# A four-layer sparse graph network: sums ahead of the tail's steps, reciprocals from PSUM, and the next block's queries at chosen tail steps

## Chip, cores and metric

The kernel runs on one core of one Trainium2 chip. The metric is the device time of one execution in microseconds. Before the change three executions took 2613.1 (median), 2613.42 and 2607.16 us.

## What is computed

Sixteen sequences of 1024 nodes with 128 features pass through four layers, all with one 1024 x 1024 adjacency matrix whose entries are 1 with probability 0.0078 (about 8 neighbours per node). Layers 0, 2 and 3 are masked attention blocks, layer 1 is a graph attention with one score per edge. Biases and norms' gains are inputs.

```python
# attention layer (0, 2, 3); 8 heads of 16
scores = einsum('bnhd,bmhd->bhnm', Q, K) / 4
scores = where(adj == 0, -inf, scores)
out = einsum('bhnm,bmhd->bnhd', softmax(scores), V)
x = layer_norm(h + out @ Wo + bo)
x = layer_norm(x + relu(x @ W1 + b1) @ W2 + b2)

# graph layer (1)
h = x @ W
e = leaky_relu((h @ a_src)[:, :, None] + (h @ a_dst)[:, None, :], 0.2)
y = softmax(where(adj == 0, -inf, e)) @ h + x
x = layer_norm(y)
```

## The kernel before

Nodes are sorted by degree and dealt to 8 row blocks of 128 nodes. The 16 sequences are two groups of 8. A **unit** is one layer, one group and one row block: 4 x 2 x 8 = 64 units, worked through in that order. In this document they are also called blocks. Inside a unit the neighbours of its nodes are taken in **parts**: each part gathers, by indirect DMA on GpSimd (L856), the key and value rows of up to two slots per node. The last part of a unit is a half-filled one, for leftovers ("MIX"). An attention unit has 5 parts, the one of row block 0 has 7.

VectorE does three steps per part: `products` multiplies the gathered keys by the repeated queries (L868, tile pr), `exponentials` reduces over a head (L891), with the exponential on ScalarE (L895), and `weighted` multiplies the gathered values by the exponentials (L919). TensorE sums the weighted rows by node with matmuls against 0/1 matrices `marks`: `summed` (L935, tile acc) for values, two parts at once where they belong to one round. At the end of a unit `divided` sums the exponentials in the same way into a PSUM bank (den), ScalarE copies them (L971, tile both), VectorE takes the reciprocal (L973) and multiplies (L976, tiles o, two halves). GpSimd adds both to `seen`, a check on range.

A unit's **tail** then runs beside the next unit's parts, for both halves h = 0 and 1, the second one step behind. It is a generator of 15 steps in an attention layer:

1. turn o (L596, copy L598) and add the bias to x (L640)
2. output projection into ybanks (L644, L645)
3. squares for the norm's variance, on ScalarE (L580)
4. power -1/2 on GpSimd (L586)
5. scale, ScalarE (L589)
6. turn and evict with gain and shift (L596, L600, tile x)
7. first feed-forward matmuls (L655) and relu (L659)
8. second feed-forward (L664, L668)
9. to 11. squares, power and scale again
12. turn and evict (L600, tile xT)
13. and after: projection to the next layer's keys and values in steps (L538 or L558, copies L542, L559 and their like, then a store). In the last layer there are a second turn (tile outs) and an indirect store by GpSimd (L625) instead.

The steps that hold no matmul are 3 to 5 and 9 to 11.

**Fronts**: `queries(u + 1)` makes the next unit's repeated queries in four steps, for each half a matmul with Wq and its copy (L819, L823), then four matmuls that repeat rows (L828) with four copies (L831, tile qr). **Loads** bring the unit after that, and `slow` is work of layer 0 for the second group.

All of these are written into five in-order instruction queues by one loop over the parts, under a manual schedule: the program's order is the order on each engine. `others()` is called three times per part of an attention layer. Each call adds `pace[1]` to a counter, which advances all tails by a step whenever it reaches 1, and then makes one step of the first of fronts, loads or slow. The pace spreads 15 steps over a unit's calls. In iteration i of the loop, i counts parts; the calls stand as follows before the change: products(i), others, summed(i-2) and perhaps the start of `divided`, exponentials(i), others, weighted(i-1), gathers for part i+3; if a unit is closing, the rest of its tails and the end of `divided`; others.

PSUM has four rotating banks for `bank()`, two ybanks for projections, and one acc. A new bank waits until the readers of the one four allocations earlier are done. A product tile pr has four buffers, so a part's product waits for the sum over the part four earlier.

Lines are those of the kernel before. The change shifts later lines by up to 14.

Of the kernel before, what the change touches and what calls it, by code (L numbers as in the profile page):

```python
# [108 lines left out]
STEPS = 15  # L109
# [13 lines left out]
def sparse_path(ctx: ExitStack, tc: tile.TileContext, a: dict, out: bass.AP, flag):  # L123


    nc = tc.nc
# [71 lines left out]
    val_i, part = some(J, QUADS, dtype=I32), some(J, QUADS, dtype=I32)  # L198
# [559 lines left out]
    units = [(l, g, t) for l in range(len(LAYERS)) for g in range(GR) for t in range(T)]  # L758
    parts = []
# [9 lines left out]
    def is_attention(u):  # L769
        return LAYERS[units[u][0]][1] is ATTN  # L770
# [28 lines left out]
    def queries(u):  # L799

        l, g, t = units[u]
        if not is_attention(u):
            ps = bank([P, J + 1, G])
            for j in range(J):
                nc.tensor.matmul(ps[:, j, :], rep_of(j, True), srcs[g, t], start=True, stop=True)
            for k, j in enumerate(SHARED[t]):
                at = slice(64 * k, 64 * k + 64)
                nc.tensor.matmul(
                    ps[at, MIX, :], rep_of(j, True)[:, at], srcs[g, t], start=True, stop=True
                )  # L810
            ofs[u] = smalls.tile([P, J + 1, G], F32, tag="of", name="of")
            nc.scalar.copy(ofs[u], ps)
            return
        qs[u] = reps.tile([P, J, ROW], F32, tag="qr", name="qr")
        for h in range(HF):
            q = ones_.tile([P, GH * D], F32, tag="q", name="q")
            ps = bank([P, GH, D])
            for i in range(GH):
                nc.tensor.matmul(  # L819
                    ps[:, i, :], xs[l, g, t][:, h, i, :], w[LAYERS[l][0], "Wq"],  # L820
                    start=True, stop=True,
                )
            nc.scalar.copy(q, ps.rearrange("p g d -> p (g d)"))  # L823
            yield
            pss = []
            for j in range(J):
                ps = bank([P, GH * D])
                nc.tensor.matmul(ps, rep_of(j), q[32 * j : 32 * j + 32], start=True, stop=True)  # L828
                pss.append(ps)
            for j in range(J):  # L830
                nc.scalar.copy(qs[u][:, j, h * GH * D : (h + 1) * GH * D], pss[j])  # L831
            yield
# [130 lines left out]
    def divided(u):  # L963

        l, g, t = units[u]
        heads, d = (H, HD) if is_attention(u) else (1, D)
        den = bank([P, G * heads])
        for n, c in enumerate(sum(PIECES[t], [])):
            marked(t, c, den, exs[u][:, n, :])
        both = smalls.tile([P, 2, G * heads], F32, tag="both", name="both")  # L970
        nc.scalar.copy(both[:, 0, :], den)  # L971
        yield
        nc.vector.reciprocal(both[:, 1, :], both[:, 0, :])  # L973
        for h in range(HF):
            o = twos.tile([P, GH, D], F32, tag="o", name="o")
            nc.vector.tensor_tensor(  # L976
                o.rearrange("p g (a d) -> p (g a) d", d=d),
                accums[u][:, h, :].rearrange("p (a d) -> p a d", d=d),
                both[:, 1, h * GH * heads : (h + 1) * GH * heads]
                .rearrange("p (a o) -> p a o", o=1)  # L980
                .to_broadcast([P, GH * heads, d]),
                ALU.mult,
            )
            tails.append((attention_tail if heads > 1 else graph_tail)(l, g, t, h, o))
        n = G * heads
        nc.gpsimd.tensor_tensor(seen[:, :, :n], seen[:, :, :n], both, ALU.add)

    tails = []
    fronts = []
    loads = []  # L990
# [4 lines left out]
            if next(gen, "end") == "end":  # L995
                gens.remove(gen)

    pace = [0.0, 0.0]

    def idle():  # L1000
        return slow if held[0] or not busy[0] else []

    def others():
        pace[0] += pace[1]
        while pace[0] >= 1.0:
            advance(tails)
            pace[0] -= 1.0
        for gens in (fronts or loads or idle(),):
            if not gens:
                continue  # L1010
            got = next(gens[0], "end")
            if got == "end":
                gens.pop(0)
            if got == "idle":
                advance(idle())

    with tc.manual_schedule():
        wide = [gather_buffer() for _ in range(EDGES)]
        setup, entry, weights = graph(wide), at_once(0), load_weights("L0")
        next(setup)  # L1020
        next(weights)
        next(entry)
        more = [weights, load_graph_weights()]
        rest = slots()
        for i, room in enumerate(setup):
            if i == T:
                for gen in more:
                    next(gen)
            if room == "load":
                for _ in loaded(0):  # L1030
                    next(entry, None)
            elif room == "queries":
                for _ in entry:
                    pass
                for _ in queries(0):
                    pass
            elif isinstance(room, str):
                next(rest)
            else:
                for _ in range(room):  # L1040
                    next(entry, None)
        for _ in entry:
            pass
        scratch.close()
        prods = ctx.enter_context(tc.tile_pool(name="prods", bufs=4))
        smalls = ctx.enter_context(tc.tile_pool(name="smalls", bufs=3))
        slow.append(at_leisure(1))
        for i in range(AHEAD - 1):
            gathered(i)
        nc.gpsimd.memset(wide[3], 0.0)  # L1050
        gathered(AHEAD - 1)
        fronts.extend([rest, loaded(1)] + more)
        closing = None
        begun = 0
        for i in range(len(parts) + 2):
            here = i < len(parts)
            u = parts[i][0] if here else len(units)
            if here:
                l = units[u][0]
                if i and parts[i - 1][0] != u:  # L1060
                    begun = i
                    if l + 1 < len(LAYERS) and LAYERS[l + 1][1] is ATTN:
                        if units[u][1:] == (0, 1):
                            more = load_weights(LAYERS[l + 1][0])
                            next(more)
                            next(more)
                        if units[u][1:] == (0, 4):
                            next(more, None)
                if is_attention(u):
                    products(i)  # L1070
            others()
            if i > 1:
                summed(i - 2)
                done = parts[i - 2][0]
                if parts[i - 1 : i] == [] or parts[i - 1][0] != done:
                    closing = divided(done)
                    next(closing)
            if here:
                exponentials(i)
            if here and i == begun + 1:  # L1080
                if is_attention(u):
                    shared(u)
                while loads:
                    advance(loads)
                if u + 1 < len(units):
                    fronts.append(queries(u + 1))
                loads.append(loaded(u + 2))
                if units[u + 2 : u + 3] and units[u + 2][0]:
                    advance(loads)
            others()  # L1090
            if 0 < i <= len(parts):
                weighted(i - 1, 0)
                if not is_attention(parts[i - 1][0]):
                    others()
                    weighted(i - 1, 2)
                gathered(i - 1 + AHEAD)
            if closing is not None and here:
                while tails:
                    advance(tails)
                for _ in closing:  # L1100
                    pass
                closing = None
                passes = 3 if is_attention(u) else 4
                steps = STEPS if is_attention(done) else GRAPH_STEPS
                pace[:] = 0.0, steps / (passes * sum(part[0] == u for part in parts) - 1)
            others()
            if i + 1 >= len(parts) or parts[i + 1][0] != u:

                while fronts:
                    advance(fronts)  # L1110
        while tails:
            advance(tails)
        for _ in closing:
            pass
        while tails:
            advance(tails)
# [434 lines left out]
```

## Time and profile before

| | us |
|---|---|
| median of three runs | 2613.1 |
| profiled execution | 2568.43 |
| its span, first to last instruction | 2566.7 |
| TensorE busy | 2105.7 (82%) |
| VectorE busy | 1931.2 (75%) |
| ScalarE busy | 1480.3 (58%) |
| GpSimd busy | 1454.9 (57%) |
| mean granted TensorE clock | 0.914 |

The profiled execution is one of its own, 1.7% below the median of the three timed ones. By time the layers lie at about 190 to 896 us (layer 0), 896 to 1201 (layer 1), 1201 to 1900 (layer 2) and 1900 to 2530 (layer 3). Ahead of them the graph is sorted. A line of the waits reads: who waited, for whom, us in total, how often, the longest. A line of the timeline has start, duration, engine, line, operation, output from inputs and shapes, the count of merged rows, and in brackets the idle time ahead with what ended it. A matmul of these float32 tiles shows as two rows.

### The profile page before, as it was taken

What the parts mean: (1) busy time and instruction counts of PE and PEld (TensorE: products, weight loads), DVE (VectorE), ACT (ScalarE), POOL (GpSimd) and SP (SyncE); (2) the same over time, 40 slices, a digit from 0 to 9 for tenths busy, and PEclk for the clock granted to TensorE, in tenths of its full rate; (3) what the DMA queues carried; (4) which work ended last, traced back from release to release, by engine and by line L of the source; (5) the groups of instructions that cost most, each with busy time, mean ns of one, the idle gap of its engine ahead of it and who ended that gap; (6) DMA issues with size and microseconds to landing.
All of it is one profiled execution on the core that took longest, in us unless ns stands there. A gap on an engine that the chain in (4) does not pass through costs nothing. (4 is left out here: it accounts for less than half of the span.)

```text
span 2566.7 us, 36698 instructions
## 1 busy us (share of the span) xinstructions
PE 2105.7 (82%) x13124; PEld 1297.6 (51%) x13124; DVE 1931.2 (75%) x1470; ACT 1480.3 (58%) x4640; POOL 1454.9 (57%) x978
## 2 busy tenths in 40 slices
PE   6558888788887898888788888988888787788776
PEld 5425655545554554454455554555555444455444
DVE  7887687587878476567887879888797787877781
ACT  3226676566665554455476666666666565556654
POOL 3335555356665688685554556555565565566561
PEclk8679999899988999999899999999999898889898
DMA  7656777567767598888787877778776767576750
GB/s 242 240 178 235 280 274 276 201 229 256 244 246 243 175 338 305 283 308 298 275 280 246 293 254 268 262 264 294 258 262 249 249 215 259 198 245 223 255 191 18
DMA packets 168463, 636.07 MB, mean 248 GB/s; under 512 B 38328, under 2 KB 41144, under 8 KB 119774
## 3 DMA queue, kind: packets, MB, share of 16 engines
q0 software_dynamic: 92672, 485.09, 53.7%
q1 hardware_dynamic: 75600, 148.55, 17.3%
q8 instruction: 105, 1.72, 0.3%
q14 instruction: 86, 0.70, 0.1%
HBM read 603.11 MB, written 92.34 MB: 271 GB/s over the span
## 5 line engine op out<-in xcount | busy, mean ns | idle before, releaser
L856 POOL DMA_INDIRECT e<-table,idx x600 | 961.3, 1602 | 580.0 <-DVE pr L919 355.3
L919 DVE TENSOR_TENSOR pr<-e,ex 128x2048 f32<-128x2048 f32 (+1 forms) x336 | 689.8, 2061 | 161.8 <-ACT ex L895 138.5
L868 DVE TENSOR_TENSOR pr<-e,qr 128x2048 f32<-128x2048 f32 x204 | 461.1, 2260 | 152.5 <-PE acc L935 85.3
L891 DVE TENSOR_REDUCE sc<-pr 128x128 f32<-128x2048 f32 (+1 forms) x252 | 518.5, 2058 | 8.6
L586 POOL TENSOR_TENSOR rstd<-total,power 128x4 f32<-128x4 f32 x224 | 327.8, 1465 | 326.2 <-ACT z L580 312.5
L935 PE MATMUL acc<-pr,marks 128*32 128x512 f32 x2656 | 487.0, 610 | 31.1 <-DVE pr L919 31.1
L580 ACT ACTIVATE z<-yps,root 128x128 f32<-128x128 f32 x896 | 317.7, 376 | 124.1 <-PE yps L668 68.0
L596 PE MATMUL ps<-ident,z 128*128 128x128 f32 x896 | 208.0, 334 | 162.1 <-ACT z L589 161.6
L589 ACT ACTIVATE z<-yps,rstd 128x128 f32<-128x128 f32 x896 | 255.9, 378 | 92.2 <-POOL rstd L586 89.3
L596 PEld LDWEIGHTS ps<-ident,z 128*128 128x128 f32 x896 | 134.0, 157 | 346.1 <-ACT z L589 251.0
L655 PE MATMUL ps<-x,W 128*128 128x512 f32 x384 | 247.9, 781 | 32.3 <-ACT x L600 32.3
L659 ACT ACTIVATE f<-ps,b 128x512 f32<-128x512 f32 x192 | 132.2, 690 | 232.6 <-PE ps L655 232.5
L664 PE MATMUL yps<-W,f 128*128 128x128 f32 x1536 | 256.5, 285 | 11.2 <-ACT f L659 8.5
L538 PE MATMUL ps<-Wkv,xT 128*128 128x256 f32 x768 | 223.4, 425 | 32.4 <-ACT xT L600 26.7
L935 PEld LDWEIGHTS acc<-pr,marks 128*32 128x32 f32 x2656 | 100.5, 110 | 280.2 <-issue 224.8
L664 PEld LDWEIGHTS yps<-W,f 128*128 128x128 f32 x1536 | 211.4, 196 | 56.1 <-ACT f L659 37.2
L831 ACT COPY qr<-ps 128x512 f32<-128x512 f32 x384 | 196.6, 600 | 53.4 <-PE ps L828 52.9
L580 ACT ACTIVATION_READ_ACCUMULATOR z<-yps,root 128x1 f32 x896 | 193.4, 216 | 0.0
L538 PEld LDWEIGHTS ps<-Wkv,xT 128*128 128x128 f32 x768 | 146.1, 208 | 80.3 <-ACT xT L600 44.6
L644 PE MATMUL yps<-Wo,oT 128*128 128x128 f32 x768 | 159.2, 290 | 6.0 <-ACT oT L598 6.0
L645 PE MATMUL yps<-centre,x 128*128 128x128 f32 x768 | 156.6, 286 | 6.4
L542 ACT COPY kv<-ps 128x512 f32<-128x512 f32 x176 | 103.6, 590 | 89.7 <-PE ps L538 86.1
(159 smaller groups left out, 2644.4 us busy)
## 6 DMA issues: line engine op xcount, KB each, us to landing
table<-kv SPq DMA_DIRECT2D x88, 512.0 KB, 10.6
qx<-qr SPq DMA_DIRECT2D x96, 256.0 KB, 9.4
kept<-xT SPq DMA_DIRECT2D x96, 256.0 KB, 5.0
x<-kept SPq DMA_DIRECT2D x48, 512.0 KB, 9.1
e<-table,idx POOLq DMA_INDIRECT x600, 8.1
table<-kv SPq DMA_DIRECT2D x32, 256.0 KB, 11.0
edges<-in_adj SPq DMA_DIRECT2D x8, 512.0 KB, 4.9
spare<-in_x SPq DMA_DIRECT2D x8, 512.0 KB, 6.6
```

The source lines that it names most:

```text
L538: nc.tensor.matmul(ps[:, k, :], x[:, i + k, :], w[LAYERS[l][0], "Wkv"], start=True, stop=True,)
L580: nc.scalar.activation(z[:, i, :], y[:, i, :], AF.Square, scale=D**-0.5, bias=root, accum_out=total[:, i : i + 1],)
L586: nc.gpsimd.tensor_tensor(rstd, total, power, ALU.pow)
L589: nc.scalar.activation(z[:, i, :], y[:, i, :], AF.Copy, scale=rstd[:, i : i + 1])
L596: nc.tensor.transpose(ps[:, i, :], z[:, i, :], ident)
L655: nc.tensor.matmul(ps, p["W1"][:, f * P : (f + 1) * P], x1.rearrange("p g n -> p (g n)"), start=True, stop=True,)
L664: nc.tensor.matmul(ps[:, i, :], f1[:, f, i * P : (i + 1) * P], p["W2"][:, f, :], start=(f == 0), stop=False,)
L856: nc.gpsimd.indirect_dma_start(out=es[i][:, k, :], out_offset=None, in_=tables[l, g][:, :], in_offset=bass.IndirectOffsetOnAxis(ap=idx[:, ...
L868: nc.vector.tensor_tensor(prs[i][0][:, :n, :], es[i][:, :n, :ROW], qx[u].rearrange("p (o c) -> p o c", o=1) if (MIX, 0) in piece else of_p ...
L891: nc.vector.tensor_reduce(sc[:, :n, :], prs[i][0][:, :n, :].rearrange("p k (a d) -> p k a d", d=HD), mybir.AxisListType.X, ALU.add,)
L919: nc.vector.tensor_tensor(prs[i][k0 // 2][:, :m, :].rearrange("p k (a d) -> p k a d", d=d), es[i][:, k0 : k0 + m, base : base + ROW].rearr ...
L935: nc.tensor.matmul(outs[32 * j : 32 * j + 32], marks[:, mark, :], rhss, start=(r == 0 and chunk[0] != MIX), stop=(chunk == last),)
```

## The change

Three edits. First, `divided` no longer copies the sums before the reciprocal: the reciprocal reads the PSUM bank, and the copy to `both` comes after the tails have been made. Second, in the loop the first `others()` of a part moves from ahead of the sums to behind them, so that the sums of part i-2, and the start of `divided`, precede that call's tail and front steps. Third, from layer 1 on, `queries(u + 1)` joins fronts at the first part of unit u instead of the second, and its four steps wait for a count of tail steps: at least 10 and 11 in the tail that is running, then 4 and 5 in the next (`ROOM`; STEPS is 15). While a front waits, loads go on. In layer 0 the queries join as before and do not wait.

```diff
@@ divided
-        nc.scalar.copy(both[:, 0, :], den)
         yield
-        nc.vector.reciprocal(both[:, 1, :], both[:, 0, :])
+        nc.vector.reciprocal(both[:, 1, :], den)
...
             tails.append((attention_tail if heads > 1 else graph_tail)(l, g, t, h, o))
+        nc.scalar.copy(both[:, 0, :], den)
         n = G * heads
         nc.gpsimd.tensor_tensor(seen[:, :, :n], seen[:, :, :n], both, ALU.add)
@@ others
-    pace = [0.0, 0.0]
+    pace = [0.0, 0.0, 0, 0]
+    ROOM = (10, 11, STEPS + 4, STEPS + 5)
+    left = []
...
             advance(tails)
             pace[0] -= 1.0
-        for gens in (fronts or loads or idle(),):
+            pace[2] += 1
+        wait = fronts and left and pace[2] < left[0]
+        if fronts and not wait and left:
+            left.pop(0)
+        for gens in ((not wait and fronts) or loads or idle(),):
@@ the loop over parts
                     begun = i
+                    if u + 1 < len(units) and l:
+                        fronts.append(queries(u + 1))
+                        left[:] = [pace[3] + k for k in ROOM]
...
                     products(i)
-            others()
             if i > 1:
                 summed(i - 2)
                 done = parts[i - 2][0]
                 if parts[i - 1 : i] == [] or parts[i - 1][0] != done:
                     closing = divided(done)
                     next(closing)
+            others()
...
-                if u + 1 < len(units):
+                if u + 1 < len(units) and l == 0:
                     fronts.append(queries(u + 1))
...
                 closing = None
+                pace[3] += STEPS
+                pace[2] = pace[3]
...
-                pace[:] = 0.0, steps / (passes * sum(part[0] == u for part in parts) - 1)
+                pace[:2] = 0.0, steps / (passes * sum(part[0] == u for part in parts) - 1)
```

In the built program of a layer-2 unit this gives the following orders (shortened; x4 and x8 are instructions).

```
TensorE before: sums of ex; L538 x2; Wq; turn o; L828 x4; yps; turn o; Wq; yps; L828 x4; acc x8;
                turn z; L655; turn z; L664; L655; L664; acc x8; turn z; L538 x2; turn z; L538 x4; acc x4
TensorE after:  sums of ex; L538 x6; turn o; yps; turn o; yps; Wq; acc x8; L828 x4;
                turn z; L655; turn z; L664; L655; L664; acc x8; Wq; turn z; L828 x4; L538 x2; turn z; acc x4
ScalarE after, at each norm: squares x8, q copy and scale (in one order or the other), L831 x4,
                evict; before, one L831 x4 stood ahead of the yps and one between the squares
```

## The prediction

> **What bounds the kernel now.** I read the busy table first. No engine is full: TensorE 82%, VectorE 75%, and matmul busy time is modelled.
>
> ```profile
> PE 2105.7 (82%) x13124; PEld 1297.6 (51%) x13124; DVE 1931.2 (75%) x1470; ACT 1480.3 (58%) x4640; POOL 1454.9 (57%) x978
> ```
>
> The chain that ended last holds only the final 4 us, so I went to the waits of VectorE:
>
> ```profile
> DVE both L973 <- ACT both L971: 152.3, 57, 11.9
> DVE pr L919 <- ACT ex L895: 138.5, 63, 8.2
> DVE pr L868 <- PE acc L935: 99.2, 28, 9.5
> ```
>
> These 390 us are what the change touches. I cut the trace into blocks, from reciprocal to reciprocal. An attention block takes 39 to 43 us, of which VectorE works 32.4. First to fourth layer below are layers 0 to 3. Where one of the three waits is short another is long (third layer: 1.3 + 3.3 us in a block of 39.2, or 4.8 + 0 in one of 40.7), so the period is set elsewhere: by the tail of the block before, which runs through TensorE, ScalarE and GpSimd in their fixed orders. The stages:
>
> ```profile
> core 0: us, PE busy (x) PEld busy (x) DVE busy (x) ACT busy (x) POOL busy (x), PEclk, DMA share, GB/s
> 190.00:896.00 706.00, 588.97 (x3788) 375.60 (x3789) 507.02 (x300) 441.38 (x1457) 391.79 (x262) 0.94 0.70 242
> 896.00:1201.00 305.00, 273.43 (x1781) 152.77 (x1780) 201.22 (x250) 151.34 (x536) 234.35 (x177) 0.96 0.88 310
> 1201.00:1900.00 699.00, 610.58 (x3722) 372.24 (x3721) 580.84 (x332) 443.43 (x1335) 387.46 (x245) 0.93 0.78 267
> 1900.00:2530.00 630.00, 502.36 (x3183) 303.75 (x3183) 488.67 (x279) 376.86 (x1164) 367.95 (x236) 0.91 0.64 225
> ```
>
> One block of the third layer, by TensorE and then ScalarE:
>
> ```profile
> 1749.68 1.10 PE L596 MATMUL ps<-ident,z 128*128 128x128 f32 x4 [2.18 <-ACT z L589]
> 1751.65 3.56 PE L655 MATMUL ps<-x,W 128*128 128x512 f32 x4 [0.87 <-ACT x L600]
> ```
>
> ```profile
> 1745.66 2.05 ACT L831 COPY qr<-ps 128x512 f32<-128x512 f32 x4 [0.89 <-PE ps L828]
> ...
> 1749.26 1.14 ACT L589 ACTIVATE z<-yps,rstd 128x128 f32<-128x128 f32 x4
> 1750.27 0.33 ACT L895 ACTIVATE ex<-sc 128x128 f32<-128x128 f32 x1
> 1750.82 0.78 ACT L600 ACTIVATE x<-ps,ln_b,ln_g 128x512 f32<-128x512 f32 x1 [0.22 <-PE ps L596]
> ```
>
> The reader is to see a serial run: scale (L589), turn (L596), evict (L600), feed-forward (L655), with TensorE idle before it, and L655 at 3.56 us where the same four rows take 1.88 at 1758.54: the clock has halved. In the fourth layer GpSimd sets when the run starts:
>
> ```profile
> 2361.12 2.87 POOL L625 DMA_INDIRECT out<-outs,places  x1 [0.30 <-issue]
> 2369.34 0.99 POOL L625 DMA_INDIRECT out<-outs,places  x1 [5.35 <-ACT qr L831]
> ...
> 2377.33 3.70 POOL L586 TENSOR_TENSOR rstd<-total,power 128x4 f32<-128x4 f32 x2
> ```
>
> The second store waits for the first (its semaphores include the first's DMA), and the norm's power stands behind both; its scale then waits 2.38 us for it.
>
> [...] 33 half-clock stretches in the last two layers, 102.4 + 109.2 us, in steps of 3.41, after windows with (mostly) under 1.5 us of matmul. [...] in the trace every ScalarE row starts in program order. [...] no row before shows a reciprocal from PSUM.
>
> **The change part by part.** I compared the two programs' order by engine. VectorE, GpSimd and SP keep theirs and no DMA is added; TensorE and ScalarE change.
>
> *Reciprocal from PSUM.* It takes ScalarE's copy (0.21 us and its hop: sums end 1734.75, reciprocal 1735.11) off the path: 0.36 becomes about 0.15. [...] So 0.15 us per block on VectorE, which is not the bound. The copy now stands after the rest of the next-layer projection. Two things wait for it: seen on GpSimd, behind which the next gather waits for VectorE 8.7 us anyway (cover), and the PSUM bank of the sums, which in the third layer the turn of o needs, and in the first the query matmul: TensorE stands about 1 us there. I charge it below.
>
> *Sums first.* The sums pass the last projection step (third layer: two steps of 1.13 us), so the reciprocal comes earlier; those steps then stand before the turn of o, so TensorE's own sequence is no shorter. The sum that releases products (3.26 us waits) still follows L664 directly in the last two layers: no gain. First layer: six L558 in a row, then the bank: +0.4 us (0.8 of stall, less the 0.43 that the turn waits for o), where gathered rows do not hide it. Fourteen blocks: +6 us, bounds -15 (1 us per block if the earlier VectorE brings the gathers forward) and +10. Second layer: GpSimd issues without a break of over 0.3 us; 0, within 6.
>
> *Queries moved.* Eight copies (L831, 0.60 each), two q copies and their matmuls leave the yps part of the tail and go to its norms. Nothing is added to the sum of work. But on ScalarE four copies now stand between scale and evict, twice per block.
> Third layer, from the end of the sums: reciprocal 0.15, weighting 8.8 (8.66 after it, as now), gathers and power 13.2 (4.41 after it, as now), scale 14.3 to 15.4 (now 14.5). Then four copies 2.05, exponential 0.33, evict 0.78: L655 starts at 18.6 instead of 16.9. At full clock it ends at 20.5, as now (20.46 at half clock); at half clock 22.2. The matmuls that moved fill only TensorE's time up to 16.5, so 2.1 us of idle stay and the clock may go either way. At the second norm the q matmul (1.06) stands before the turn, and the fourth bank from the copies holds the sums: +0.64. With the later start at the end: 39.6 or 41.3 us instead of 38.8. I take +1.6, 13 blocks (not the two seven-piece ones, VectorE 42 busy, nor the edge): +21, bounds +10 and +33.
> Fourth layer: the second norm's copies (2.05) and q put the first output eviction at 6.5 us after the sum instead of 3.4; the first store starts at 6.5, not 4.86: +1.65, and with it the second store, the gathers and power. Then the copies again: evict starts 3.5 us after scale, not 1.70: +1.8. Together +3.45 with L655 slow as now; if fast 1.9 less. The idle before it grows, so I expect slow mostly: +3.0, 13 blocks: +39, bounds +20 and +45. The weighting of that part, which had its exponential in time, then waits some 3 us: that wait is late next.
>
> Sum: 6 + 0 + 21 + 39 = +66 us. The profiled execution took 2568.4 (span 2566.7), giving 2634; the three runs' median is 2613.1, 1.7% above that execution, and I put the difference on it: **2679**. Own range of this case, from the bounds (+9 to +94): 2622 to 2707.
>
> **Rivals.** *Faster by the clock:* [...] L655 takes 1.88 instead of 3.56 in 26 blocks: 26 x 1.7 = 44 us, 2569. For it: 212 us at half clock lie in exactly these layers, and the waits of 2.18 and 4.42 are where matmuls go. Against: the copies follow the scale in order, so new idle opens. It decides if the copies' cost per block is under 1.7 us.
> *No change:* 152 us of reciprocal waits end, and the same wait appears at the next product or exponential, while gains and copies cancel: 2613. For it: the blocks with different waits and like lengths. Against: the first store's delay has no cover.
> *The change does not do what it says:* sums first moves no sum, since TensorE arrives late in either order; then only the queries count: 21 + 39 = +60, 2673, inside my case.
>
> **How the numbers follow.** Slower 0.78; the clock 0.14; no change 0.08. A measurement of this kernel can tell 0.3% (8 us). Most of the slower case lies above 2621. Range 2600 to 2720: it takes in no change and the shallow part of the clock rival.
>
> **What would show it.** Right: evict L600 of x starts 3.3 us or more after its scale with four L831 between; the first L625 store later against the sum; waits for the exponential longer; reciprocal waits below 100 us and ended by TensorE; half-clock time still over 150 us in the last two layers. Wrong: L655 near 1.9 us everywhere, fourth-layer blocks under 41 us, or the copies done before the scale.

## The result and the profile after

The changed kernel took 2638.4 us (median of four, 2633.3 to 2652.3) beside 2610.4 us for the kernel before (2607.2 to 2613.4): a ratio of **1.0116 [1.0074, 1.0157]** (in brackets, here and below, the 95% interval), +28 us. The forecast was 2679 us, +66. The sign is right and the time lies in the range; the size is not.

First the busy table of the changed kernel, against which the one of before is to be held:

```profile
PE 2117.7 (80%) x13124; PEld 1306.8 (50%) x13124; DVE 1932.4 (73%) x1470; ACT 1467.7 (56%) x4640; POOL 1468.3 (56%) x978
```

VectorE works 1932.4 us instead of 1931.2. Nothing was added to it, so whatever time the change costs must stand in its waits. These are its three longest (who waited, for whom, us in total, how often, the longest):

```profile
DVE pr L919 <- ACT ex L895: 249.3, 82, 10.9
DVE pr L868 <- PE acc L935: 93.9, 25, 10.5
DVE both L972 <- PE ps L935: 90.7, 45, 9.0
```

The reciprocal's wait fell from 152.3 to 90.7 us, and TensorE ends it now. The wait of the weighting (L919) for its exponential rose from 138.5 to 249.3. That is where the time went, and the cost group of the turns shows who holds it:

```profile
L596 PE MATMUL ps<-ident,z 128*128 128x128 f32 x896 | 190.1, 331 | 166.0 <-ACT qr L831 104.2
```

A turn of z (the matmuls that transpose it into a PSUM bank, from which ScalarE evicts it) needs the scaled z, yet 104.2 us of the idle time ahead of these turns are ended by a query copy. One block of layer 2 (the prediction's third layer), ScalarE and then TensorE from the timeline, shows why:

```profile
1741.23 1.14 ACT L589 ACTIVATE z<-yps,rstd 128x128 f32<-128x128 f32 x4 [2.58 <-POOL rstd L586]
1742.25 2.06 ACT L831 COPY qr<-ps 128x512 f32<-128x512 f32 x4
1744.15 0.38 ACT L895 ACTIVATE ex<-sc 128x128 f32<-128x128 f32 x1
1744.36 0.83 ACT L600 ACTIVATE x<-ps,ln_b,ln_g 128x512 f32<-128x512 f32 x1
```

```profile
1742.91 0.76 PE L596 MATMUL ps<-ident,z 128*128 128x128 f32 x4 [2.52 <-ACT qr L831]
1745.25 3.78 PE L655 MATMUL ps<-x,W 128*128 128x512 f32 x4 [1.58 <-ACT x L600]
```

Four copies stand between scale and evict. Evict starts 3.13 us after its scale (1741.23 to 1744.36); in the block of before that the prediction shows it was 1.56 (1749.26 to 1750.82). Two things hold evict there. Its turn starts only 1.68 us after the scale: the idle time ahead of it (2.52 us) is ended by the first copy, which gives a PSUM bank back. And ScalarE, which in this trace starts its instructions in program order, has the copies ahead of evict until 1744.31 in any case. The experiments below move both at once and don't tell them apart. The feed-forward L655 starts 18.75 us after the end of the sums (1726.50), for which the prediction had 18.6; and it runs at half clock: 3.78 us at a granted clock of 0.50, where the prediction has 1.88 us for the same four rows at another place.

**A pair of profiles that misleads.** The profiled executions took 2568.4 us before and 2638.1 after, +70, which looks like the forecast's +66 to the us. It is not: as the experiments show, the kernel before takes 2573 to 2585 us on some chips and 2606 to 2610 on others, and its first profile (2568.4) lies at the lower level while its first timed runs (2613.1) lie at the upper. All comparisons by layer below use kernels of one chip.

### The profile page after: what moved, and what is told of

The parts are those of the page before. It is cut to its first block, busy times and chain, and to the rows that moved or that the text cites. A ratio compares the mean times of both kernels' runs of the same rounds, so it can differ in the third digit from the quotient of the medians.

```text
span 2636.4 us, 36645 instructions
## 1 busy us (share of the span) xinstructions
PE 2117.7 (80%) x13124; PEld 1306.8 (50%) x13124; DVE 1932.4 (73%) x1470; ACT 1467.7 (56%) x4640; POOL 1468.3 (56%) x978
## 5 line engine op out<-in xcount | busy, mean ns | idle before, releaser
L856 POOL DMA_INDIRECT e<-table,idx x600 | 931.2, 1552 | 518.5 <-DVE pr L919 304.8
L919 DVE TENSOR_TENSOR pr<-e,ex 128x2048 f32<-128x2048 f32 (+1 forms) x336 | 689.2, 2060 | 282.4 <-ACT ex L895 249.3
L868 DVE TENSOR_TENSOR pr<-e,qr 128x2048 f32<-128x2048 f32 x204 | 462.0, 2265 | 137.7 <-PE acc L935 81.5
L586 POOL TENSOR_TENSOR rstd<-total,power 128x4 f32<-128x4 f32 x224 | 343.5, 1537 | 364.9 <-ACT z L580 363.0
L935 PE MATMUL acc<-pr,marks 128*32 128x512 f32 x2656 | 503.8, 622 | 41.8 <-DVE pr L919 38.8
L596 PE MATMUL ps<-ident,z 128*128 128x128 f32 x896 | 190.1, 331 | 166.0 <-ACT qr L831 104.2
L655 PE MATMUL ps<-x,W 128*128 128x512 f32 x384 | 251.1, 789 | 49.6 <-ACT x L600 48.6
L538 PE MATMUL ps<-Wkv,xT 128*128 128x256 f32 x768 | 205.1, 411 | 24.2 <-ACT xT L600 10.6
L644 PE MATMUL yps<-Wo,oT 128*128 128x128 f32 x768 | 166.1, 300 | 47.5 <-ACT oT L598 47.5
L580 ACT ACTIVATION_READ_ACCUMULATOR z<-yps,root 128x1 f32 x896 | 187.9, 210 | 0.0
L645 PE MATMUL yps<-centre,x 128*128 128x128 f32 x768 | 165.3, 299 | 9.6
```

What stands on the lines that cost most here:

```text
L538: nc.tensor.matmul(ps[:, k, :], x[:, i + k, :], w[LAYERS[l][0], "Wkv"], start=True, stop=True,)
L580: nc.scalar.activation(z[:, i, :], y[:, i, :], AF.Square, scale=D**-0.5, bias=root, accum_out=total[:, i : i + 1],)
L586: nc.gpsimd.tensor_tensor(rstd, total, power, ALU.pow)
L596: nc.tensor.transpose(ps[:, i, :], z[:, i, :], ident)
L655: nc.tensor.matmul(ps, p["W1"][:, f * P : (f + 1) * P], x1.rearrange("p g n -> p (g n)"), start=True, stop=True,)
L856: nc.gpsimd.indirect_dma_start(out=es[i][:, k, :], out_offset=None, in_=tables[l, g][:, :], in_offset=bass.IndirectOffsetOnAxis(ap=idx[:, ...
```

## The experiments

Three edits are told apart: **R**, the reciprocal from PSUM with the copy behind the multiplies; **S**, sums ahead of the waiting steps; **Q**, the queries with ROOM.

### Is it the chip, the profiler or the change?

The kernel before, unchanged, in the first set:

> The kernel before, unchanged, for a second profile. The forecast was made from an execution of 2568 us, while the timed runs of the same kernel take 2607 to 2613. Theory A (the kernel has more than one clock pattern, and the profiled execution was a lucky one): the new profile lies near 2610, its blocks keep their VectorE and ScalarE durations, and the 40 us are in TensorE time at half clock: about 80 us more of it than the 420 of the first profile, mean granted clock near 0.90 instead of 0.914. Theory B (the profiler changes the time): this profile lies near 2568 again while the timed runs lie at 2610.

2580.9 us (2566 to 2592) beside 2576.2 (2567 to 2589), ratio 1.0016 [1.0000, 1.0032]; its profiled run took 2576.1. So the profile adds nothing, and not one of 44 runs on this chip comes near 2610. The changed kernel in the second set, on another chip:

> The changed kernel as it stands, timed beside the kernel before on the chip of this call. Theory A (the sum over the layers was right, and it was put on a base that does not belong to it): where the kernel before takes about 2576 us, this takes about 2640, +60 to +70 us, a ratio of 1.023 to 1.027. Theory B (the change is worth only +28 us wherever it is timed, and the profiled execution exaggerates it): a ratio of 1.009 to 1.014, about 2604 us.

2633.9 us beside 2608.1 (2598 to 2623): 1.0098 [1.0071, 1.0126]. Here the change costs 26 us. Then both, on a third chip:

> The kernel before, unchanged. In the first set of experiments it took 2576 us (2567 to 2589), in the second 2608 us (2598 to 2623): the two sets were run on different chips, and the ranges do not meet. Theory A (each chip has its own level for this kernel): its profiled execution here lies within 10 us of the median of this set, near 2576 or near 2608. Theory B (one chip takes both levels at different times): times of both kinds within this set, a spread of over 30 us.

> The changed kernel once more. It took 2638 and 2634 us where the kernel before took 2610 and 2608. If this set's chip has the lower level for the kernel before (2576): theory A, the change costs the same part everywhere, 2600 to 2606, ratio 1.009 to 1.013; theory B, the changed kernel takes the same time on both chips and what it costs depends on the chip, 2632 to 2640, ratio 1.022 to 1.025. If the chip has the upper level, 2630 to 2640 again, ratio 1.008 to 1.012, and the pair of profiles of one chip shows in which layers the 28 us lie: by the sum of the prediction, scaled, nothing in layer 1, a third in layer 2, most in layer 3.

The kernel before took 2577.8 beside 2572.8, 1.0012 [0.9996, 1.0028]. Within each set of runs the kernel keeps to one level, and each set ran on a chip of its own; as no chip came twice, it is inferred, not shown, that the level belongs to the chip. The changed kernel took 2615.8 us, 1.0141 [1.0102, 1.018]: +43 us, between the two theories. So the forecast's +66 is too large at either level, and its fault isn't the median on which it was put.

### The parts by themselves

R and S with the queries as before, on the first and the third chip:

```diff
-        nc.scalar.copy(both[:, 0, :], den)
         yield
-        nc.vector.reciprocal(both[:, 1, :], both[:, 0, :])
+        nc.vector.reciprocal(both[:, 1, :], den)
...
+        nc.scalar.copy(both[:, 0, :], den)
...
-            others()
             if i > 1:
                 summed(i - 2)
...
+            others()
```

> Two of the three edits: reciprocals from PSUM and sums first; queries as before. Theory A (the queries' copies carry the loss): faster than before or equal, 2595 to 2612; layer 0 shorter by about 10 us as in the profile of the full change, layers 2 and 3 within 0.5 us per block of before. Theory B (the copy kept back holds a PSUM bank and the projection stands ahead of the turn of o): slower by 0.6 to 1 us per attention block, 2630 to 2650.

> Sums first and the reciprocal from PSUM alone, again; it measured 0.989 beside a kernel before of 2576 us. Theory A (the same gain on every chip): 0.986 to 0.992. Theory B (it gains more on the upper level, where the kernel with the early copy measured 0.978): 0.974 to 0.982.

2545.7 us both times: 0.989 [0.9852, 0.9929] and 0.9887 [0.9846, 0.9928]. This half of the change is a gain of 27 to 31 us, where the prediction had a loss of 6. (That is more than the first expectation's first theory has, -15 to +2 us on a base of 2610; the second one's first theory holds.) Q alone, on the same two chips:

```diff
-    pace = [0.0, 0.0]
+    pace = [0.0, 0.0, 0, 0]
+    ROOM = (10, 11, STEPS + 4, STEPS + 5)
...
+                    if u + 1 < len(units) and l:
+                        fronts.append(queries(u + 1))
+                        left[:] = [pace[3] + k for k in ROOM]
...
-                if u + 1 < len(units):
+                if u + 1 < len(units) and l == 0:
```

> The queries' edit alone; the copy before the reciprocal and the calls in their old place. Theory A (the four copies between scale and evict on ScalarE): 2630 to 2660, blocks of layers 2 and 3 at 41 to 43 us, evict L600 of x starting 3.3 us or more after the scale. Theory B (bank and order of the sums): within 8 us of before.

> The queries part alone, again; it measured 1.037 beside a kernel before of 2576 us. Theory A (its cost is the copies on ScalarE, the same on every chip): 1.034 to 1.039. Theory B (its cost depends on the chip, and on the upper level it is smaller, as the +28 us of the whole change suggests): 1.022 to 1.030.

2669.0 and 2674.3 us: 1.0369 [1.0313, 1.0424] and 1.0363 [1.0314, 1.0412], +93 and +102 us, more than the first expectation had (at most 2660 us, on a base of 2610). On top of R and S the same edit cost less, 2615.8 - 2545.7 = 70 us. The third chip has a profile of all four, and cutting each at the reciprocals of units 0, 15, 30, 31, 47 and 62 gives these stretches in us:

| | to unit 0 | layer 0 | layer 1 | unit 30 | layer 2 | layer 3 | end | span |
|---|---|---|---|---|---|---|---|---|
| before | 187.6 | 668.5 | 324.2 | 22.8 | 656.1 | 642.9 | 82.2 | 2584.3 |
| R and S | 190.7 | 661.9 | 315.3 | 26.8 | 646.6 | 629.4 | 77.2 | 2548.0 |
| Q | 192.2 | 667.2 | 324.2 | 26.2 | 700.3 | 685.9 | 78.1 | 2674.1 |
| all three | 191.9 | 655.7 | 329.2 | 28.1 | 683.2 | 660.0 | 74.1 | 2622.2 |

Layers 2 and 3 by engine, from the windows of before, and then of the full change (columns: window, length, busy time of TensorE, weight loads, VectorE, ScalarE, GpSimd, clock, DMA share, GB/s; the second pair's windows start about 1 us after the reciprocals):

```profile
1203.10:1859.20 656.10, 566.86 (x3478) 348.98 (x3477) 538.89 (x309) 416.19 (x1251) 364.18 (x230) 0.92 0.78 268
1859.20:2502.10 642.90, 521.72 (x3228) 312.28 (x3226) 507.87 (x283) 383.35 (x1178) 398.90 (x241) 0.90 0.66 234
```

```profile
1205.90:1889.10 683.20, 565.98 (x3478) 344.89 (x3479) 538.86 (x308) 409.97 (x1251) 364.05 (x230) 0.93 0.75 258
1889.10:2549.10 660.00, 521.15 (x3216) 319.02 (x3214) 508.53 (x283) 378.46 (x1175) 382.40 (x241) 0.89 0.66 227
```

These are single executions; four profiles of the kernel before differ by up to 11 us in layer 3 (632 to 643), 9 in layer 1 (317 to 325) and 2 in layer 2. Busy times agree within 7 us on every engine but GpSimd, which shows 398.90 and 382.40 us in layer 3. On VectorE the 27 and 17 us are all idle time. Where they stand in a block shows this table, means over eight five-part blocks of layer 2 and nine of layer 3, read from the timelines, in us from the start of the block's reciprocal ("rest" is from the second norm's evict to the next reciprocal). The blocks are those of units 33, 36, 41 to 46, 49 to 53 and 57 to 60; over all 14 and 13 five-part blocks the last column reads 40.36, 39.49, 43.07, 41.87 and 42.12, 40.90, 45.02, 43.32, the same picture:

| | turn of o | power | scale | evict | L655, its length | second evict | rest | block |
|---|---|---|---|---|---|---|---|---|
| layer 2, before | 1.50 | 13.08 | 14.43 | 16.03 | 16.86, 3.65 | 32.87 | 7.01 | 39.88 |
| R and S | 2.82 | 13.01 | 15.63 | 17.27 | 18.10, 3.10 | 33.62 | 5.42 | 39.04 |
| Q | 1.50 | 13.07 | 14.42 | 17.54 | 18.42, 2.98 | 33.86 | 8.63 | 42.49 |
| all three | 2.51 | 13.01 | 14.35 | 17.48 | 18.37, 3.68 | 35.11 | 6.19 | 41.30 |
| layer 3, before | 1.44 | 13.83 | 16.69 | 18.40 | 19.23, 3.73 | 34.95 | 6.88 | 41.83 |
| R and S | 1.42 | 14.74 | 16.78 | 18.48 | 19.31, 3.78 | 35.49 | 5.48 | 40.97 |
| Q | 1.40 | 13.37 | 16.52 | 19.64 | 20.53, 2.98 | 35.88 | 9.13 | 45.01 |
| all three | 1.43 | 14.05 | 16.69 | 19.82 | 20.71, 3.76 | 37.48 | 5.76 | 43.24 |

Two things are to be read. Q lengthens the way from scale to evict by 1.4 to 1.5 us, with or without R and S, and moves the second evict back by 0.9 to 1.0 us alone and 1.5 to 2.0 on top of R and S; alone it also lengthens the rest by 1.6 to 2.3, where the sums stand behind those late steps. R and S shorten the rest by 1.4 to 1.6, and with Q by 2.4 to 3.4. In the whole block they gain 0.84 and 0.86 us without Q, 1.19 and 1.77 with it (over all five-part blocks 0.87 and 1.22, 1.20 and 1.70): the parts don't add up, and here lies most of why Q costs 70 us in their company and 93 to 102 alone.

How the rest gets shorter, in one block of layer 3; the kernel before, TensorE and the reciprocal:

```profile
2070.94 0.66 PE L596 MATMUL ps<-ident,xT 128*128 128x128 f32 x4 [0.87 <-ACT xT L600]
2071.52 0.62 PE L935 MATMUL acc<-pr,marks 128*32 128x512 f32 x2
2073.26 0.50 PE L935 MATMUL ps<-ex,marks 128*32 128x64 f32 x12
2074.13 0.55 DVE L973 RECIPROCAL both<-both 128x64 f32<-128x64 f32 x1 [0.54 <-ACT both L971]
```

and the kernel with R and S:

```profile
2046.58 0.62 PE L935 MATMUL acc<-pr,marks 128*32 128x512 f32 x2
2048.32 0.51 PE L935 MATMUL ps<-ex,marks 128*32 128x64 f32 x12
2048.76 0.66 PE L596 MATMUL ps<-ident,xT 128*128 128x128 f32 x4
2050.07 0.55 DVE L972 RECIPROCAL both<-ps 128x64 f32<-128x64 f32 x1
```

Before, the sums wait for the last turn, which itself waits 0.87 us for an evict, and VectorE, idle for 0.54 us, starts the reciprocal 0.36 us after the sums, behind the copy. After, the turn stands behind the sums, the sums end 1.24 us before the reciprocal (2048.83 against 2050.07), and the reciprocal has no wait: it starts when VectorE is through with the weighting ahead of it. In layer 3 with R and S eight of 14 reciprocals stand 1.24 us behind their sums like this one; five follow them by 0.1 us.

VectorE is busy for 1931 to 1934 us in all four kernels of the third chip, so their spans differ by its waits. The five largest, which follow the spans to within 14 us, for the reciprocal, the exponential, the sum of products, and gathered rows at scores (L900) and products (L868), in us:

| | reciprocal | exponential | acc | rows, L900 | rows, L868 | sum | span |
|---|---|---|---|---|---|---|---|
| before | 157.5 | 140.9 | 98.8 | 64.3 | 62.8 | 524.3 | 2584.3 |
| R and S | 59.7 | 174.0 | 95.8 | 79.0 | 67.8 | 476.3 | 2548.0 |
| Q | 213.3 | 177.2 | 122.0 | 67.2 | 37.0 | 616.7 | 2674.1 |
| all three | 97.2 | 241.9 | 90.8 | 80.0 | 38.2 | 548.1 | 2622.2 |

R and S end 98 us of reciprocal waits and get 33 back at the exponential and 20 at gathered rows.

### R or S, and the bank

On a fourth chip, of the upper level (before 2606.4), four kernels side by side: S alone, R alone, both, and both with the copy of den early in the program (the edit against R and S):

```diff
+        nc.scalar.copy(both[:, 0, :], den)
         yield
         nc.vector.reciprocal(both[:, 1, :], den)
...
-        nc.scalar.copy(both[:, 0, :], den)
```

> Only the order: the sums and the start of divided ahead of the waiting steps; the copy still stands between the sums and the reciprocal, the queries as before. Theory A (the gain is the order: from the second norm's evict to the reciprocal it took 5.4 to 5.5 us with both edits and 6.9 to 7.0 before): 0.987 to 0.993. Theory B (it is the copy that no longer stands ahead of the reciprocal): 0.996 to 1.001.

> Only the reciprocal from PSUM with the late copy; it measured 0.9944 on the chip where the kernel before takes 2608. Theory A (a saving of 0.2 to 0.3 us a block ahead of the reciprocal, which the block's period follows): 0.993 to 0.997 on any chip. Theory B (a gain of that chip alone): 0.998 to 1.001.

> Both edits together, 0.989 twice where the kernel before takes 2573 to 2576. On a chip of that level again 0.987 to 0.991. If the product of e13's and e14's ratios comes to this, the two gains are independent.

> Both edits, the copy early. Theory A (the bank held by the late copy costs about 1 us a block in layers 0 and 2): 20 to 30 us below e15. Theory B (it costs nothing, and the 0.978 measured before is the other chip's level): within 5 us of e15.

S: 2561.4 us, 0.9807 [0.9762, 0.9851]. R: 2591.6, 0.9947 [0.9928, 0.9966]. Both: 2550.5, 0.9787 [0.9754, 0.982]; the product of the single ratios, 0.9755, lies at the edge of its interval. So at the upper level the order carries most of the gain, three quarters or more. What R adds to S, 11 us, is no larger than these four-run medians leave open. At the lower level, where both gain 27 to 31 us and not 56, S and R were not run alone.

With the early copy it took 2549.1 us, 0.9781 [0.9749, 0.9812], 1.4 us from the late one. By its second theory the bank costs nothing, but that is not shown. (The 20 to 30 us of the first are also more than the prediction's own charge, 0.4 us in 14 blocks.) In the early kernel all 64 reciprocals start after the copy has ended, though they don't read it, and 31 wait for it (S alone: 35 for 95.4 us):

```profile
DVE both L973 <- ACT both L971: 66.8, 31, 9.2
```

The copy and the reciprocal write one tile, `both`, which is probably the reason, though no run tests it. So the early copy gives the bank back and brings the copy's wait back, and the pair shows only that the two together come to nothing. The wait is worth about 15 us by an estimate (the reciprocals that wait follow the sums by 0.36 us with it and by 0.12 without, 64 times); so the bank may be worth as much. It also makes this kernel S alone but for what the reciprocal reads, and it measured 12 us below S: so much the medians leave open.

An earlier pair had told less, R alone and the early copy on the second chip:

> Only the reciprocal from PSUM, with the copy of den moved behind the multiplies; sums and queries stand where they stood before. Sums first and the reciprocal from PSUM together measured 0.989. Theory A: the gain lies in the copy that no longer stands between the sums and the reciprocal, so this alone gives nearly all of it, 0.988 to 0.993. Theory B: it lies in issuing the sums ahead of the waiting steps, and this alone gives little, 0.997 to 1.003.

> Sums first and the reciprocal from PSUM, queries as before, but the copy of den stays ahead of the reciprocal in program order, so that den's PSUM bank is given back early. The prediction charged about 1 us a block in layers 0 and 2 to the bank that the late copy holds. If that charge is real, this is about 27 us below the version with the late copy: a ratio of 0.978 to 0.983. If the bank is not on the path, it is the same as that version: 0.987 to 0.992. If the early copy and the reciprocal hinder one another at the bank, above that: 0.992 to 0.998.

2593.4 us, 0.9944 [0.9927, 0.9961], between its two theories, and 2552.1 us, 0.9781 [0.9759, 0.9802]. The second looked like the charge for the bank confirmed, since 0.989 was known for the late copy; it was the level of the chip, where the late copy has 0.9787.

### Where the copies stand

If the place of the four copies is the cause, moving them ahead of the scale takes the cost away with nothing else in the program changed. A tail step earlier, which does so in the first norm only:

```diff
-    ROOM = (10, 11, STEPS + 4, STEPS + 5)
+    ROOM = (9, 10, STEPS + 3, STEPS + 4)
```

> The full change with the queries' steps tied one tail step earlier (9, 10 and 3, 4 instead of 10, 11 and 4, 5). By program order this moves, at the first norm only, the four copies L831 ahead of the scale, where ScalarE waits 2.6 us for GpSimd's power in the profile after. Theory A: evict follows scale by 1.7 us again, layers 2 and 3 gain 1.5 to 3.4 us per block (26 blocks), 2550 to 2600. Theory B (the loss comes from the bank or from the second norm): 2630 to 2650, no change.

2556.9 us, 0.9911 [0.988, 0.9943]. The full change was not run on this chip; on the third, of the same level, it took 2615.8. So some 60 us, most of what Q costs on top of R and S (70), go with the place of the first norm's copies. In the second norm four copies still stand between scale and evict. R and S without Q took 2545.7 on this chip, 11 us less, but the intervals overlap. A block of layer 2, from its timeline:

```profile
1707.35 2.06 ACT L831 COPY qr<-ps 128x512 f32<-128x512 f32 x4
1709.25 1.21 ACT L589 ACTIVATE z<-yps,rstd 128x128 f32<-128x128 f32 x4
1710.88 0.78 ACT L600 ACTIVATE x<-ps,ln_b,ln_g 128x512 f32<-128x512 f32 x1 [0.22 <-PE ps L596]
1711.71 1.98 PE L655 MATMUL ps<-x,W 128*128 128x512 f32 x4 [0.87 <-ACT x L600]
```

The copies fill the time in which ScalarE waits for GpSimd's power (2.58 us in the block of the changed kernel above). Evict follows 1.63 us after scale, and L655 takes 1.98 us, not 3.78: the clock has held. This is the prediction's clock rival, met with the copies out of the way. The mean of L655 in such blocks of layer 2 is 2.78 us, the clock of the layer 0.97 against 0.93 in the kernel before on the same chip. In layer 3 most L655 stay slow (mean 3.48 us over the five-part blocks; clock 0.92 for 0.91). How much of the 60 us is the earlier evict and how much the clock, no run tells. Last, no copies in the second norm at all, with the late and with the early copy of den:

```diff
-    ROOM = (10, 11, STEPS + 4, STEPS + 5)
+    ROOM = (STEPS, STEPS + 1, STEPS + 3, STEPS + 4)
```

> The full change with ROOM = (STEPS, STEPS + 1, STEPS + 3, STEPS + 4): two of a block's query copies go before the first norm starts, two ahead of its scale, and none falls in the second norm. With (9, 10, STEPS + 3, STEPS + 4) it was 0.991, with layer 3 7 us longer than where the queries are left as before. Theory A: that 7 us is what the copies of the second norm cost, so this gives 0.986 to 0.990, about the version with the queries as before. Theory B: the earlier copies take ScalarE from the exponentials and evictions of the output products, and it is 0.993 to 1.00.

> The full change with ROOM = (STEPS, STEPS + 1, STEPS + 3, STEPS + 4) and the copy of den ahead of the reciprocal in program order. With the late copy it was 2543 where the kernel before takes 2608. Theory A (the bank is not on the path): 2538 to 2548. Theory B (the early copy gives the turn of o its bank back sooner, and the clock holds, since copies and turns close up): 2525 to 2535.

2543.2 us on the second chip, 0.975 [0.9728, 0.9772], a lower ratio than its expectation had from the lower level, but in us about what R and S take with the queries as before (2546 to 2551); and 2532.3 us on a fifth one, 0.9809 [0.9769, 0.9849] (before 2582.3). The last is the lowest median of all, 13 us below R and S alone, though not on the same chip. Blocks of 37.0 us stand in its layer 2, its scale-to-evict is 1.64 us and L655 2.71. The expectation for it with the bank freed early (2525 to 2535) fits, but the two runs are of different chips, and here too all 64 reciprocals start after the copy and 33 wait for it: that the bank is the reason is not shown. On this chip the kernel before once more, for its level:

> The kernel before, unchanged, for a profile on a chip of the upper level if this is one. Theory A (the level lies in the wait between the second norm's evict and the reciprocal, which sums first shortens, since the kernel with both edits takes 2546 and 2550 on both levels): there the layers 2 and 3 are 5 to 15 us longer each than in the profiles of the lower level (655 and 637). Theory B (it lies in the gathers of layers 0 and 1): layers 0 and 1 are 10 us or more longer, the others the same. On a chip of the lower level (2570 to 2580) the question stays open.

2584.5 us beside 2582.3, 1.0000 [0.9987, 1.0013], the lower level again. In which layer the upper level's 30 us lie stays open, since no profile of the kernel before was taken there. The two profiles of R alone, both of the upper level, give a hint: layer 1 takes 338 us in each, for 317 to 325 in the kernel before at the lower level, and no other layer is longer. As R alone was not profiled at the lower level, they don't tell the level from R. R and S with the queries as before takes 2546, 2546 and 2551 us at both levels, which suggests that the 30 us lie in something that S takes off.

## Why the prediction was wrong, step by step

The sum beside the third chip's profiles (before to all three, us):

| step | forecast | measured |
|---|---|---|
| layer 0: sums first and the bank | +6 | -12.8 |
| layer 1, and unit 30 at its end | 0 | +5.0, +5.3 |
| layer 2: four copies twice | +21 | +27.1 |
| layer 3: store, copies | +39 | +17.1 |
| start and end | - | +4.3, -8.1 |
| sum | +66 | +37.9 |

**The step that failed: "Sums first"**, with its words "TensorE's own sequence is no shorter" and, for the last two layers, "no gain", and "VectorE, which is not the bound" for the reciprocal. The two edits together were priced at +6, all of it in layer 0. They measured -36 in the profiles (-7 in layer 0, -9 in layer 1, -10 in layer 2, -14 in layer 3) and -27 to -31 in the medians at the lower level, -56 at the upper. The argument looked at the wrong place. TensorE's sequence is indeed no shorter: in layer 2 the turn of o comes 1.3 us later after the reciprocal (1.50 to 2.82). But the sums no longer stand behind the tail's last steps, so the reciprocal comes sooner after the second evict, and the next norm isn't tied to the turn alone. Its power stands 13.0 us after the reciprocal in all four kernels of layer 2, through weighting and gathers; the prediction says so itself, in deriving the scale from the reciprocal, and then didn't use it. What is taken from ahead of the reciprocal and put behind it lies, for the most part, beside VectorE's weighting. Not wholly: with R and S alone the scale of layer 2 starts 1.2 us later (15.63), in most blocks not on its power but behind four query copies and the other half's squares, which follow the later turn. One such block, with GpSimd's power and ScalarE:

```profile
1296.64 2.05 ACT L831 COPY qr<-ps 128x512 f32<-128x512 f32 x4 [0.88 <-PE ps L828]
1297.05 1.04 POOL L586 TENSOR_TENSOR rstd<-total,power 128x4 f32<-128x4 f32 x1
1299.85 0.25 ACT L580 ACTIVATION_READ_ACCUMULATOR z<-yps,root 128x1 f32 x1
1299.94 1.20 ACT L589 ACTIVATE z<-yps,rstd 128x128 f32<-128x128 f32 x4
```

The power is done at 1298.09, the scale starts at 1299.94. With the queries moved (all three) the scale is back at 14.35. Hence, for R and S, -1.6 in the rest, +0.7 in the way to the second evict, -0.84 in the block.

**Layer 0, the bank.** The stall was right, in kind and in size: in the median of eleven five-part blocks the turn of o comes 0.65 us later (1.50 to 2.15) and the scale 0.49 (14.15 to 14.64), for a forecast of +0.4. Against it the rest falls from 6.32 to 4.61 us, which the forecast lacked, and the layer is shorter.

**Layer 2** was right in kind and nearly in size: evict +1.45 us, L655 +1.5 and at half clock as before (3.68 for 3.65), the block +1.42 for a forecast of +1.6. The layer's +27 lies inside the bounds (+10 to +33), but by luck: underneath, two errors offset, R and S with -10 and Q on top of them with +37 for +21.

**Layer 3**: of +3.0 a block, the part by the copies (+1.8) came, 1.42 in evict and 2.5 in the second evict. The other part, the first store's +1.65, did not. The stores by GpSimd, before and after:

```profile
2071.61 2.87 POOL L625 DMA_INDIRECT out<-outs,places  x1 [0.30 <-issue]
2079.72 1.00 POOL L625 DMA_INDIRECT out<-outs,places  x1 [5.23 <-ACT qr L831]
```

```profile
2104.82 1.41 POOL L625 DMA_INDIRECT out<-outs,places  x1 [1.76 <-ACT outs L598]
2111.80 0.99 POOL L625 DMA_INDIRECT out<-outs,places  x1 [5.57 <-issue]
```

By the trace the sums end at 2073.77 and 2105.96. The first store does start later against them, -1.1 instead of -2.2 us, but the second, on which by the forecast everything after it hangs, starts 5.9 and 5.8 us after them: no later. So it is over 13 blocks of the layer (all but the one that ends with unit 56's reciprocal): the first store moves from -2.2 to -1.1 us in the median, the second starts 5.2 us after the sums in both means. With R and S alone it is 7.1 and with Q alone 3.2, since the sums move too: two shifts that the forecast lacked cancel. Power (13.83 to 14.05) and scale (16.69 both) stay about where they were. The rest, 1.1 us shorter than before, gives part of the copies back: +1.41 a block. By parts, R and S gave -13.5 us and Q +30.6.

**What was right.** The queries edit as a loss and its place: forecast +60, measured +70 in company of the others (that the two numbers are so near is in part luck: +37 for +21 and +31 for +39 in the two layers). Reciprocal waits below 100 us and ended by TensorE (90.7); the exponential's wait late next (249.3); the product's wait for acc unchanged (93.9 for 99.2); half-clock time in the last two layers over 150 us (263 us between the reciprocals of units 31 and 62). The reciprocal from PSUM takes hardly longer than from `both`, before and after on the third chip by shape (busy us, mean ns, idle ahead):

```profile
L973 DVE RECIPROCAL both<-both 128x64 f32<-128x64 f32 x48 | 26.5, 552 | 126.2 <-ACT both L971 121.7 <-ACT ex L895 4.4
```

```profile
L972 DVE RECIPROCAL both<-ps 128x64 f32<-128x64 f32 x48 | 26.8, 557 | 82.9 <-PE ps L935 82.6
```

That is 5 ns more in the mean of 48. The prediction saves 0.21 us ahead of the reciprocal (0.36 to 0.15) and counts 0.15 of it; the rest was an estimate for the source in PSUM, which no trace before showed.

**The rivals.** The clock rival's condition, copies that cost less than 1.7 us a block, isn't met in this change; it is met one tail step earlier, where the clock of layer 2 was 0.97 for 0.93. That L655 gets faster by the change was the rival's assumption; on the third chip the clock of layers 2 and 3 is 0.93 and 0.89 with it, for 0.92 and 0.90 before. That sums first moves no sum is refuted by the two timelines above. The rival of no change is excluded by the interval [1.0074, 1.0157], but gains and copies do cancel in part, as it had it: -27 and +70 on the third chip.

## What to carry to other kernels

Find the instruction from which the period's later steps keep their distance, here VectorE's reciprocal, and price a moved step by which side of it it lands on; that its own engine's sequence stays as long says little. Then check what stands in order behind the moved step, as the squares here. On an engine that starts its work in program order, as ScalarE does in these traces, put copies that can wait into the hole ahead of an instruction that is waiting for another engine, not between that instruction and the one that needs its result: that place was worth some 60 us here. When an edit is to free something early, see in the trace that it does only that. And don't subtract a profile of one chip from a profile of another: here that made +70 out of +28.

## What the runs showed of the hardware

The kernel before has medians of 2573 to 2585 us on three chips and of 2606 and 2608 on two, one set of runs on each, with ranges of 2563 to 2596 and 2594 to 2623 that hardly touch, at the same mean clock (0.91). The difference of 1.2% is larger than most edits here, and it isn't the same for every kernel: the changed one differs by 0.7% (2616 and 2634), the one with R and S by 0.2% (2546 and 2551).
